# Gate's probability carried with the scattered rows and multiplied in by ScalarE; layer 0's outputs gathered by DMAs that add into x

## The chip, the cores and the metric

The kernel runs on one core of a Trainium2 chip. The metric is the time of one execution on the device in microseconds (us). An execution that the hardware profiler recorded gives a span, from the first to the last instruction, and everything that is said by engine, line or stage. The engines are called by the profile's names: PE (TensorE's matrix multiplications; PEld are its weight loads), DVE (VectorE), ACT (ScalarE), POOL (GpSimd) and SP (SyncE, which only issues DMAs here).

## What is computed

Two layers, each a graph part and a feed-forward part, on x of 128 graphs x 64 nodes x 256 channels in float32 (8192 nodes). The change lies in layer 0's feed-forward part, a mixture of eight experts of which each node takes one:

```
x = x + graph_part_0(layernorm(x), adj)
xf = layernorm(x)                               # 8192 x 256
H = gelu(xf @ W1 + b1)                          # 8192 x 1024
probs = softmax(H @ Wg + bg)                    # 8 experts
assign = argmax(probs)
out = sum over e of where(assign == e, probs[:, e] * (H @ Wd[e] + bd[e]), 0)
x = x + out
x = x + graph_attention_1(layernorm(x), adj)    # layer 1, 64 x 64 attention per graph
x = x + experts_1(layernorm(x), edge_index)     # 4 experts, two of them for each node
```

So a node's output is its expert's product, plus that expert's bias, times the largest probability of its own softmax.

## The kernel before

The 8192 nodes are 64 tiles of 128 (P); four tiles make a group (GR), so there are 16 groups. x stays in the core's own memory, SBUF, all the time (`x`, P x 64 x 256). The kernel goes through stages, and the instructions of each engine are put in order by a scheduler that works on the program when it is built: what stands later in the code can be ahead on an engine if nothing forbids it. `tc.issue_after(v)` holds an instruction behind v in that order. Buffers come from pools with a fixed number of each tile (`bufs`); who takes a buffer again waits for its last reader.

**Layer 0, groups (0 to 620 us).** `graph` does the graph part. `gated` (from L678) does the first half of the experts: it normalizes a group, multiplies by W1 with gelu (`hidden`, L457), turns the gelu rows back to one node per partition (`turned`, L705, copied by ACT into `rows`, two tiles of P x 4 x 512), and computes the gate. At L742 and L743 the largest probability of each node goes into `psel` (P x 64, kept to the end). The node's place among its expert's rows (`pos`, L768) is counted with matrix multiplications. Then POOL scatters the gelu rows by indirect DMA (L773): for each tile two DMAs, each of 128 rows of 512 floats, into the DRAM tensors `hrows0` and `hrows1`, which hold the rows sorted by expert.

**The turn to the slots (620 to 650 us).** After the last group SP fills the 128 rows past each expert's end with zeros (L837, 16 DMAs, of which each expert has two), and the last four slots' rows of `yrows` (L844). DVE computes which expert and which rows each of the slots has (`slot_e`, `slot_t`), and where each node's output will stand in `yrows` (`row_y`).

**The slots (650 to 1000 us).** A slot is 128 sorted rows of one expert; 68 are always done (`slots(0, SURE)`), four more under a condition on the device. `slots` has `load` (L939: two DMAs on SP's queue bring a slot's 128 x 1024 gelu rows into `hin`, of which there are three buffers), `turn` (PE transposes them in eight pieces, L951, four to a PSUM tile; ACT copies each four to `hTt`, L954), sixteen matrix multiplications of an expert's weights (L969; eight of them in the code, which the profile counts twice), the addition of the bias by DVE (L977), and the write of y to DRAM on SP's queue (L978). In the code load(t + 2) and turn(t + 1) stand ahead of slot t's multiplications. Beside them DVE sorts the edges' keys for layer 1 (`keys.finish`, `keys.count`), and PE counts them (L311); both are held behind the bias addition of the slot before.

**Layer 1's graph part (1001 to 1380 us).** A loop of steps (`for s in range(n_steps)`) runs five streams of groups at different lags: `back` (lag 0), `first`, `second`, `combine` and `tables`. `back(g)` brings layer 0's outputs home: for each of a group's four tiles POOL gathers 128 rows of 256 floats from `yrows` by indirect DMA into a buffer `yin` (L1180; six buffers, shared with later work), DVE multiplies it by `psel` and adds it to x (L1195), and DVE takes the sums for the normalization (`raw_stats`, L1172). The additions of some groups are held behind the factors or scores of an earlier group (`ahead`). After each pair of steps `make_factors` turns the sums into scale and shift. From step 12 on, matrix multiplications of layer 1's experts (`units`, L1101 and L1111) are put between, and after these stages PE has work to the end (2120 us).

Of the kernel before, what the change touches and what calls it, by code (L numbers as in the profile page):

```python
# [82 lines left out]
def kernel(  # L83
# [99 lines left out]
    n_left = n_chunks * n_chunk + n_firsts // PER + n_extra  # L183
    dram = ctx.enter_context(tc.tile_pool(name="dram", bufs=1, space=DRAM))
    left = dram.tile([n_left, P, PER], F32, name="left")
    hrows = [dram.tile([E0 * NROW, HALF], F32, name=f"hrows{i}") for i in range(FD // HALF)]
    yrows = dram.tile([NSLOT * P, D], F32, name="yrows")
    psel = const.tile([P, NT], F32, name="psel")
    row_y = const.tile([P, NT], I32, name="row_y")
    on = const.tile([P, NT, 64], U8, name="on")  # L190
    cnt = const.tile([P, NT], F32, name="cnt")
# [230 lines left out]
    with tc.tile_pool(name="w0", bufs=1, reuse_waits="tile") as w0, tc.tile_pool(name="kp", bufs=1, reuse_waits="tile") as kp:  # L422
# [29 lines left out]
        with tc.tile_pool(name="bg1", bufs=1, reuse_waits="tile") as bg1, tc.tile_pool(  # L452
# [19 lines left out]
            with tc.tile_pool(name="b2", bufs=1, reuse_waits="tile") as b2, tc.tile_pool(  # L472
# [205 lines left out]
                def gated(g):  # L678
# [21 lines left out]
                        S.copy(zT[:, c, :], tz)  # L700
                        yield
                    hTs = []
                    rows = [b2.tile([P, GR, HALF], F32, name=f"rows{i}") for i in range(FD // HALF)]

                    def turned(q):  # L705
                        th = psb.tile([P, GR * P], F32, name="tz")
# [32 lines left out]
                    yield  # L739
                    V.reciprocal(sm, sm)  # L740
                    V.tensor_tensor(pr, pr, sm.unsqueeze(2).to_broadcast([P, GR, E0]), ALU.mult)
                    best = psel[:, GR * g : GR * g + GR]  # L742
                    V.tensor_reduce(best, pr, AX.X, ALU.max)  # L743
                    V.tensor_tensor(pr, pr, best.unsqueeze(2).to_broadcast([P, GR, E0]), ALU.is_equal)
                    V.tensor_tensor(pr, pr, order.unsqueeze(1).to_broadcast([P, GR, E0]), ALU.mult)
                    V.tensor_reduce(m, pr, AX.X, ALU.max)
# [72 lines left out]
            with tc.tile_pool(name="bg3", bufs=1, reuse_waits="tile") as bg3:  # L819
                pk = psg0.tile([P, GR * P], F32, name="ms")  # L820
                nc.tensor.matmul(pk[:, 0:E0], ones, run[:, NG, 0, :], start=True, stop=True)
                full = bg3.tile([P, E0], I32, name="full")

                none = bg3.tile([P, D], F32, name="none")
                nc.gpsimd.memset(none, 0.0)
                V.tensor_tensor(full, pk[:, 0:E0], base, ALU.add)
                _, ends = nc.values_load_multi_w_load_instructions(
                    full[0:1, :],
                    engines=(mybir.EngineType.SP,),
                    min_val=0,  # L830
                    max_val=E0 * NROW - P,
                    skip_runtime_bounds_check_because="an expert has N nodes at most",
                )
                for e in range(E0):
                    for rows in hrows:
                        alone(
                            nc.sync.dma_start(  # L837
                                rows[bass.ds(ends[e], P), :].rearrange("p (k f) -> p k f", f=D),
                                none.unsqueeze(1).to_broadcast([P, HALF // D, D]),
                            )  # L840
                        )

                for t in range(SURE, NSLOT):
                    nc.sync.dma_start(yrows[t * P : t * P + P, :], none)  # L844
                full = bg3.tile([P, E0], I32, name="fullt")
                V.tensor_scalar(full, pk[:, 0:E0], float(P - 1), None, ALU.add)
                V.tensor_scalar(full, full, 7, None, ALU.logical_shift_right)
                tiles = bg3.tile([P, E0], F32, name="tiles")
                V.tensor_copy(tiles, full)
                end = bg3.tile([P, E0], F32, name="end")  # L850
                V.tensor_copy(end[:, 0:1], tiles[:, 0:1])
                for e in range(1, E0):
                    V.tensor_tensor(end[:, e : e + 1], end[:, e - 1 : e], tiles[:, e : e + 1], ALU.add)
                iota_s = bg3.tile([P, NSLOT], F32, name="iota_s")
                nc.gpsimd.iota(
                    iota_s, pattern=[[1, NSLOT]], base=0, channel_multiplier=0, allow_small_or_imprecise_dtypes=True
                )

                posf = bg3.tile([P, NT], F32, name="posf")
                V.tensor_copy(posf, pos)  # L860
                move = bg3.tile([P, NT], F32, name="move")
                shift = bg3.tile([P, E0], F32, name="shift_y")
                V.tensor_scalar(shift, tiles, float(P), -float(NROW), ALU.mult, ALU.add)
                V.tensor_copy(row_y, posf)
                for e in range(1, E0):
                    V.tensor_scalar(move, posf, float(e * NROW), shift[:, e - 1 : e], ALU.is_ge, ALU.mult)
                    V.tensor_tensor(row_y, row_y, move, ALU.add)

                V.tensor_scalar(more_slots, end[:, E0 - 1 : E0], float(SURE), None, ALU.is_gt)
                most = bg3.tile([P, 1], F32, name="most")  # L870
                V.tensor_scalar(most, end[:, E0 - 1 : E0], -1.0, None, ALU.add)
                V.tensor_scalar(iota_s, iota_s, most, None, ALU.min)
                past = bg3.tile([P, NSLOT, E0], BF16, name="past")
                V.tensor_tensor(
                    past,
                    iota_s.unsqueeze(2).to_broadcast([P, NSLOT, E0]),
                    end.unsqueeze(1).to_broadcast([P, NSLOT, E0]),
                    ALU.is_ge,
                )
                es = bg3.tile([P, NSLOT], F32, name="es")  # L880
                V.tensor_reduce(es, past, AX.X, ALU.add)
                V.tensor_copy(slot_e, es)
                V.tensor_tensor(past, past, tiles.unsqueeze(1).to_broadcast([P, NSLOT, E0]), ALU.mult)
                first = bg3.tile([P, NSLOT], F32, name="first")
                V.tensor_reduce(first, past, AX.X, ALU.add)
                V.tensor_tensor(iota_s, iota_s, first, ALU.subtract)
                V.scalar_tensor_tensor(es, es, float(NROW // P), iota_s, ALU.mult, ALU.add)
                V.tensor_scalar(es, es, 0.0, float(E0 * NROW // P - 1), ALU.max, ALU.min)
                last = V.tensor_copy(slot_t, es).ins
# [6 lines left out]
        if True:  # L896
            with tc.tile_pool(name="bs", bufs=3, reuse_waits="tile") as bs, tc.tile_pool(
# [15 lines left out]
                def slots(first, end):  # L913
# [3 lines left out]
                    def load(t):  # L917

                        if t % GR == 0:
# [14 lines left out]
                            )  # L934
                            for k in range(GR):
                                found[t + k] = at[k], ex[k]
                        h = loaded[t] = bz.tile([P, FD], F32, name="hin")
                        for i, rows in enumerate(tiles_of_rows):
                            nc.sync.dma_start(  # L939
                                h[:, i * HALF : i * HALF + HALF],  # L940
                                rows[bass.ds(found[t][0], 1)].rearrange("s p f -> (s p) f"),
                            )

                    def turn(t):

                        h = loaded.pop(t)
                        hT = turned[t] = bt.tile([P, NH, P], F32, name="hTt")
                        for i in range(0, NH, GR):
                            th = pst.tile([P, GR * P], F32, name="th")
                            for k in range(GR):  # L950
                                nc.tensor.transpose(  # L951
                                    th[:, k * P : k * P + P], h[:, (i + k) * P : (i + k) * P + P], ident
                                )
                            S.copy(hT[:, i : i + GR, :].rearrange("p q n -> p (q n)"), th)  # L954
# [4 lines left out]
                    for t in range(first, end):  # L959
# [15 lines left out]
                            )  # L975
                        y = bs.tile([P, D], F32, name="y")
                        add_bd = V.tensor_tensor(y, py, bd, ALU.add).ins  # L977
                        nc.sync.dma_start(yrows[t * P : t * P + P, :], y)  # L978
                        yield add_bd

# [169 lines left out]
    with ExitStack() as of_c:  # L1150
# [22 lines left out]

        def back(g):

            ys = []
            for k in range(GR):
                t = GR * g + k
                y = by.tile([P, D], F32, name="yin")
                nc.gpsimd.indirect_dma_start(  # L1180
                    y, None, yrows, bass.IndirectOffsetOnAxis(ap=row_y[:, t : t + 1], axis=0)
                )
                ys.append(y)


            if PART <= g <= FIRST:
                ahead = made["factors"]
            elif FIRST < g <= 2 * FIRST:
                ahead = made["scores"]
            else:  # L1190
                ahead = None
            for k in range(GR):
                t = GR * g + k
                with tc.issue_after(ahead) if ahead is not None else ExitStack():
                    V.scalar_tensor_tensor(x[:, t, :], ys[k], psel[:, t : t + 1], x[:, t, :], ALU.mult, ALU.add)  # L1195
                raw_stats(0, k, x[:, t, :])
                yield

        def transposed(g, norm):
# [976 lines left out]
```

## Time and profile before

| | |
|---|---|
| median of 12 executions | 2122.68 us (2118.01 to 2131.57) |
| the profiled execution | 2121.72 us, its span 2120.0 us, PE's granted clock 0.955 |
| PE | 1937.3 us busy, 91% of the span |
| PE's weight loads | 1394.6 us, 66% |
| DVE | 1341.0 us, 63% |
| ACT | 941.7 us, 44% |
| POOL | 491.3 us, 23% |
| bytes moved by DMA | 274.94 MB, mean 130 GB/s |

The shares are means over stages with different limits; by stage, in us busy:

| stretch (us) | PE | DVE | ACT | POOL | PE's clock | DMA share |
|---|---|---|---|---|---|---|
| 0 to 100 | 80.07 | 76.01 | 65.62 | 14.63 | 1.00 | 0.51 |
| 200 to 300 | 92.10 | 87.47 | 65.38 | 25.32 | 0.98 | 0.29 |
| 600 to 640 | 16.69 | 15.48 | 10.15 | 14.86 | 0.74 | 0.46 |
| 660 to 996 | 335.97 | 276.99 | 70.05 | 0.00 | 1.00 | 0.52 |
| 1001 to 1211 | 157.48 | 158.26 | 114.18 | 63.29 | 0.78 | 0.27 |
| 1300 to 1400 | 97.56 | 66.13 | 43.24 | 0.59 | 1.00 | 0.48 |
| 1800 to 2000 | 200.00 | 74.41 | 75.46 | 53.87 | 1.00 | 0.87 |

A group's line in the profile names line, engine and operation, the tile written, an arrow and the tiles read, and the count; after the bar come busy us, mean ns of one, and the idle time of the engine just before them with what ended it ("<-PE th L951" is PE's write of `th` at line 951). A line of the timeline has start and duration in us, engine, line, operation, tiles and count; in brackets the idle time before it. SPq is SP's own sequencer, whose DMA instructions are the issue of a transfer and not the transfer itself. L numbers are lines of the kernel before.

### The profile page before, as it was taken

The page shows a single profiled execution, that of the slowest core. Times are in us where ns is not written, and L with a number is a line of the kernel's source. Part 1 is how long each engine was busy: PE and PEld are TensorE (multiplying, and loading weights), DVE is VectorE, ACT ScalarE, POOL GpSimd, SP SyncE. Part 2 cuts the span into 40 slices and gives each one's busy share as a digit, 9 for nine tenths or more (in the row PEclk, how much of TensorE's full clock was granted, in tenths as well). Part 3 has the DMA queues.
Part 4 walks back from the last instruction along what each step waited for, and adds up shares of the span by engine and source line. Part 5 has one row for each costly group of instructions (what it writes and reads, how often), then busy time and mean ns, then how long its engine had stood idle before and what let it go on. Part 6 is the DMA issues. An engine that isn't in the chain of part 4 may idle for free. (4 is left out here: it accounts for less than half of the span.)

```text
span 2120.0 us, 32316 instructions
## 1 busy us (share of the span) xinstructions
PE 1937.3 (91%) x10422; PEld 1394.6 (66%) x10422; DVE 1341.0 (63%) x4346; ACT 941.7 (44%) x1721; POOL 491.3 (23%) x528
## 2 busy tenths in 40 slices
PE   7889999899957999997678999989999999999999
PEld 5444445454436989897446676757777767888876
DVE  6878988843126888885697655846778451334435
ACT  4867766766641222221365655322333333333332
POOL 2013121223220000000530100015555552303223
PEclk9999999999988999999777899999999999999999
DMA  8023222234226554544214111472222147878943
GB/s 239 27 93 118 83 96 95 87 117 165 89 111 210 153 166 153 156 157 118 76 52 136 61 43 42 142 205 62 48 58 64 42 138 250 291 255 271 293 129 100
DMA packets 229376, 274.94 MB, mean 130 GB/s; under 512 B 57937, under 2 KB 173521, under 8 KB 229201
## 3 DMA queue, kind: packets, MB, share of 16 engines
q1 hardware_dynamic: 194288, 212.26, 32.4%
q0 software_dynamic: 24064, 60.22, 9.0%
q8 instruction: 88, 1.44, 0.3%
q10 hardware_dynamic: 10848, 0.30, 0.3%
q14 instruction: 88, 0.71, 0.1%
HBM read 159.40 MB, written 113.22 MB: 129 GB/s over the span
## 5 line engine op out<-in xcount | busy, mean ns | idle before, releaser
L464 PE MATMUL ph<-zT,w 128*128 128x512 f32 x512 | 250.2, 614 | 4.8 <-ACT zT L700 3.4
L969 PE MATMUL py<-wd,hTt 128*128 x1088 | 247.4, 381 | 0.0
L969 PEld LDWEIGHTS py<-wd,hTt 128*128 128x128 f32 x1088 | 202.7, 191 | 25.0
L954 ACT COPY hTt<-th 128x512 f32<-128x512 f32 x136 | 73.2, 589 | 299.6 <-PE th L951 299.6
L1578 POOL DMA_INDIRECT got<-tsrc,esrc x144 | 152.2, 1057 | 213.0 <-DMA zslots<-none 84.5
L1111 PE MATMUL py<-w,hT 128*128 128x256 f32 x800 | 192.6, 392 | 9.3 <-DVE y L1115 5.2
L773 POOL DMA_INDIRECT hrows<-rows,pos x128 | 126.6, 989 | 307.1 <-issue 188.7
L1101 PE MATMUL ph<-zT,w 128*128 128x512 f32 x400 | 184.1, 601 | 0.0
L1111 PEld LDWEIGHTS py<-w,hT 128*128 128x128 f32 x800 | 151.5, 194 | 40.8 <-issue 11.4
L1180 POOL DMA_INDIRECT yin<-yrows,row_y x64 | 63.3, 989 | 489.1 <-SPq L1024 370.5
L464 PEld LDWEIGHTS ph<-zT,w 128*128 128x128 f32 x512 | 94.7, 197 | 105.9 <-issue 89.4
L1105 ACT ACTIVATE hT<-ph,b 128x512 f32<-128x512 f32 x100 | 68.6, 687 | 185.0 <-PE ph L1101 176.5
L2055 ACT ACTIVATE hT<-ph,b1e 128x256 f32<-128x256 f32 x152 | 71.9, 473 | 173.0 <-PE ph L2051 101.7
L2051 PE MATMUL ph<-zTp,w1e 128*128 128x256 f32 x608 | 137.6, 379 | 3.7 <-DMA w1e<-in_L_ffn_W_dram 3.7
L2064 PE MATMUL py<-w,hT 128*128 x608 | 137.5, 379 | 0.0
L2072 DVE TENSOR_TENSOR y<-py,b2e 128x256 f32<-128x256 f32 x76 | 32.1, 424 | 152.5 <-PE py L2064 136.7
L2051 PEld LDWEIGHTS ph<-zTp,w1e 128*128 128x128 f32 x608 | 115.4, 190 | 19.8 <-issue 4.3
L626 PE MATMUL pre<-wd 128*128 128x512 f32 x256 | 123.9, 601 | 1.8 <-ACT wd L612 1.3
L2064 PEld LDWEIGHTS py<-w,hT 128*128 128x128 f32 x608 | 112.7, 190 | 13.8
L467 ACT ACTIVATE hT<-ph,b 128x512 f32<-128x512 f32 x128 | 87.8, 686 | 76.1 <-PE ph L464 60.3
L1101 PEld LDWEIGHTS ph<-zT,w 128*128 128x128 f32 x400 | 73.4, 191 | 71.4 <-issue 70.3
L201 DVE TENSOR_TENSOR one<-iota_l,pb 128x2048 bf16<-128x2048 bf16 x96 | 116.6, 1214 | 0.2
(411 smaller groups left out, 3779.2 us busy)
## 6 DMA issues: line engine op xcount, KB each, us to landing
hin<-hrows SPq DMA_DIRECT2D x136, 256.0 KB
w1e<-in_L_ffn_W_dram SPq DMA_DIRECT2D x38, 512.0 KB
yin<-ystore SPq DMA_DIRECT2D x24, 512.0 KB
ystore<-y SPq DMA_DIRECT2D x80, 128.0 KB
zslots<-none SPq DMA_DIRECT2D x38, 256.0 KB
zin<-zslots SPq DMA_DIRECT2D x38, 256.0 KB
yslots<-y SPq DMA_DIRECT2D x76, 128.0 KB
bd<-in_L_ffn_bd_dram SPq DMA_DIRECT2D x68, 128.0 KB
```

What stands on the lines that cost most here:

```text
L201: V.tensor_tensor(o, numbers.unsqueeze(1).to_broadcast(shape), of.rearrange("p (j e) -> p j e", e=2).unsqueeze(2).to_broadcast(shape), ALU ...
L464: nc.tensor.matmul(ph, w1[:, c, q * P : q * P + P], zT[:, c, :], start=(c == 0), stop=(c == 1))
L467: gelus.append(S.activation(hT, ph, AF.Gelu, bias=b1[:, q : q + 1]).ins)
L626: nc.tensor.matmul(pre, xnT[:, c, n * P : n * P + P], wcat[:, c, :], start=(c == 0), stop=(c == 1),)
L773: nc.gpsimd.indirect_dma_start(to, bass.IndirectOffsetOnAxis(ap=pos[:, t : t + 1], axis=0), of[:, k, :], None)
L954: S.copy(hT[:, i : i + GR, :].rearrange("p q n -> p (q n)"), th)
L969: nc.tensor.matmul(py, hT[:, q, :], wd[:, bass.ds(e, 1), q, :].rearrange("p e f -> p (e f)"), start=(q == 0), stop=(q == NH - 1),)
L1101: nc.tensor.matmul(ph, w1[:, e, c, q * P : q * P + P], zT[:, c, :], start=(c == 0), stop=(c == 1))
L1111: nc.tensor.matmul(py, hTs[q][:, k * P : k * P + P], w2[:, e, q, :], start=(q == 0), stop=(q == NH1 - 1))
L1578: nc.gpsimd.indirect_dma_start(got, None, tsrc, bass.IndirectOffsetOnAxis(ap=esrc[:, b, at : at + 1], axis=0))
L2051: nc.tensor.matmul(ph, w1e[:, c, q * P : q * P + P], zT[:, c, :], start=(c == 0), stop=(c == 1))
L2064: nc.tensor.matmul(py, hTs[q][:, k * P : k * P + P], w2[:, e, q, :].rearrange("p e f -> p (e f)"), start=(q == 0), stop=(q == NH1 - 1),)
```

## The change

`hrows1` and its row tile become one float wider (513), and the added column holds the node's largest probability: it is copied there from `best`, a small tile that replaces `psel`, and so goes out with the scatter. The zero fill of the rows past an expert's end is done for the old columns as before and, by eight further DMAs, for the added column. A slot's load brings 1025 columns; after the bias has been added ACT multiplies y by the last column of the slot's rows, and then y is written. `loaded.pop(t)` moves from `turn` to that place. In `back` the gather's target is x itself, with an addition in the DMA; the buffers `yin`, DVE's multiplication and addition, and the order that held them are gone there, and the sums that remain are held in their place.

```diff
-    hrows = [dram.tile([E0 * NROW, HALF], F32, name=f"hrows{i}") for i in range(FD // HALF)]
+    wide = [HALF + (i == FD // HALF - 1) for i in range(FD // HALF)]
+    hrows = [dram.tile([E0 * NROW, n], F32, name=f"hrows{i}") for i, n in enumerate(wide)]
     yrows = dram.tile([NSLOT * P, D], F32, name="yrows")
-    psel = const.tile([P, NT], F32, name="psel")
...
-                    rows = [b2.tile([P, GR, HALF], F32, name=f"rows{i}") for i in range(FD // HALF)]
+                    rows = [b2.tile([P, GR, n], F32, name=f"rows{i}") for i, n in enumerate(wide)]
...
-                    best = psel[:, GR * g : GR * g + GR]
+                    best = bg2.tile([P, GR], F32, name="best")
                     V.tensor_reduce(best, pr, AX.X, ALU.max)
+                    V.tensor_copy(rows[-1][:, :, HALF], best)
...
                     for rows in hrows:
                         alone(
                             nc.sync.dma_start(
-                                rows[bass.ds(ends[e], P), :].rearrange("p (k f) -> p k f", f=D),
+                                rows[bass.ds(ends[e], P), 0:HALF].rearrange("p (k f) -> p k f", f=D),
                                 none.unsqueeze(1).to_broadcast([P, HALF // D, D]),
                             )
                         )
+                    alone(nc.sync.dma_start(hrows[-1][bass.ds(ends[e], P), HALF : HALF + 1], none[:, 0:1]))
...
-                        h = loaded[t] = bz.tile([P, FD], F32, name="hin")
+                        h = loaded[t] = bz.tile([P, FD + 1], F32, name="hin")
                         for i, rows in enumerate(tiles_of_rows):
                             nc.sync.dma_start(
-                                h[:, i * HALF : i * HALF + HALF],
+                                h[:, i * HALF : i * HALF + wide[i]],
                                 rows[bass.ds(found[t][0], 1)].rearrange("s p f -> (s p) f"),
                             )
...
-                        h = loaded.pop(t)
+                        h = loaded[t]
...
                         add_bd = V.tensor_tensor(y, py, bd, ALU.add).ins
+                        prob = loaded.pop(t)[:, FD : FD + 1]
+                        S.activation(y, y, AF.Copy, scale=prob)
                         nc.sync.dma_start(yrows[t * P : t * P + P, :], y)
...
-            ys = []
             for k in range(GR):
                 t = GR * g + k
-                y = by.tile([P, D], F32, name="yin")
                 nc.gpsimd.indirect_dma_start(
-                    y, None, yrows, bass.IndirectOffsetOnAxis(ap=row_y[:, t : t + 1], axis=0)
+                    x[:, t, :],
+                    None,
+                    yrows,
+                    bass.IndirectOffsetOnAxis(ap=row_y[:, t : t + 1], axis=0),
+                    compute_op=ALU.add,
                 )
-                ys.append(y)
...
             for k in range(GR):
-                t = GR * g + k
                 with tc.issue_after(ahead) if ahead is not None else ExitStack():
-                    V.scalar_tensor_tensor(x[:, t, :], ys[k], psel[:, t : t + 1], x[:, t, :], ALU.mult, ALU.add)
-                raw_stats(0, k, x[:, t, :])
+                    raw_stats(0, k, x[:, GR * g + k, :])
                 yield
```

## The prediction

> **What bounds the kernel now.** I read the page first, then busy time by stage, then the timeline of the stages that the diff touches: the turn from layer 0's first part to its experts (620 to 650 us), the 68 slots (650 to 1000 us) and the start of layer 1 (1001 to 1211 us, where the outputs are gathered).
>
> ```profile
> L954 ACT COPY hTt<-th 128x512 f32<-128x512 f32 x136 | 73.2, 589 | 299.6 <-PE th L951 299.6
> L1180 POOL DMA_INDIRECT yin<-yrows,row_y x64 | 63.3, 989 | 489.1 <-SPq L1024 370.5
> ```
>
> ```profile
> 850.00:900.00 50.00, 50.00 (x478) 45.06 (x477) 42.42 (x106) 10.74 (x20) 0.00 (x0) 1.00 0.52 154
> 1000.00:1050.00 50.00, 24.98 (x92) 16.38 (x92) 29.48 (x105) 14.81 (x33) 29.75 (x30) 0.66 0.28 82
> 1050.00:1100.00 50.00, 37.02 (x152) 23.85 (x152) 45.91 (x156) 34.69 (x66) 18.11 (x18) 0.90 0.17 48
> ```
>
> The columns of the second fence are the stretch, its length, busy us of PE, PE's weight loads, DVE, ACT and POOL, then granted clock, DMA share and GB/s. In the slots PE never rests (50.00 of 50 us at clock 1.00), and ACT is idle four fifths of the time, always waiting for PE. From 1050 to 1100 us DVE is the full engine (45.91 of 50). So time taken from DVE there is worth something, and work given to ACT in the slots looks free, by its share. One slot in the timeline:
>
> ```profile
> 851.30 1.07 PE L951 MATMUL th<-ident,hin 128*128 128x128 f32 x8
> 851.70 0.41 DVE L977 TENSOR_TENSOR y<-py,bd 128x256 f32<-128x256 f32 x1
> 852.03 1.07 ACT L954 COPY hTt<-th 128x512 f32<-128x512 f32 x2 [3.77 <-PE th L951]
> 852.13 0.33 SPq L978 DMA_DIRECT2D yrows<-y  x1
> 852.21 3.62 PE L969 MATMUL py<-wd,hTt 128*128 x16
> 852.71 0.86 SPq L939 DMA_DIRECT2D hin<-hrows  x2
> 853.78 0.34 SPq L966 DMA_DIRECT2D bd<-in_L_ffn_bd_dram  x1
> ```
>
> A slot lasts 5.04 us: the writes of y go from 659.20 to 996.7 us, 67 steps. What is to be seen is the order: PE turns a slot one slot before it multiplies it, and SP sends a load as soon as the turning has freed a buffer. In the order of the built program, SP sends the load of slot t+5 after y of slot t is written, and PE turns slot t+2 ahead of multiplying t+1. A load has more than two slots to land, and no slot past the second waits for one.
>
> **The slots, after.** hin has 3 buffers. Before, hin of slot t is free once PE has turned it. Now ACT's multiplication by its last column reads it, and that comes after slot t's matmuls. The order of the changed program shows what follows. SP: write of y(t), then load(t+3). ACT: both copies of slot t+2, then the multiplication of slot t. PE: matmuls of t+2, then (in part just inside them) the turning of t+3. Every link is real: load(t+3) needs the buffer that multiplication t frees; multiplication t stands behind the copies of t+2; those need the turning, and so the landing, of load(t+2). So load, turn, copy, multiply, write and next load form a ring that is run once **per slot**. Its length, from SP's write of y:
>
> - write of y to the next load's start: 852.13 to 852.71, 0.58 us.
> - that start to the landing of the load's second half. Nearest rows:
>
> ```profile
> 646.51 3.03 SPq L939 DMA_DIRECT2D hin<-hrows  x6
> 649.24 2.79 PE L951 MATMUL th<-ident,hin 128*128 128x128 f32 x12 [9.98 <-DMA hin<-hrows]
> ```
>
> ```profile
> 1763.36 0.41 SPq L2022 DMA_DIRECT2D w1e<-in_L_ffn_W_dram  x1
> 1767.70 3.69 PE L2051 MATMUL ph<-zTp,w1e 128*128 128x256 f32 x16 [3.74 <-DMA w1e<-in_L_ffn_W_dram]
> ```
>
> The first 256 KB half let PE go 2.73 us after its issue; the second is issued 0.53 us later (0.86 for two, 0.33 for one), so 3.26 us if it takes no longer. The 512 KB of w1e took 4.34 us. I take the middle, 3.8.
> - four transposes and the way to ACT: 851.30 to 852.03, 0.73 us.
> - second copy to the multiplication's start: 1.07 less 0.59, 0.48 us.
> - the multiplication, 128x256: 0.47 us, as the same Copy with a scale takes at L634; between 0.40 (a plain copy, L1127) and 0.60 (L1069).
> - ACT's end to SP: 852.11 to 852.13, 0.02 us.
> - late issues: 13 of the 68 pairs of loads took 1.05 to 2.37 us in place of 0.86, 11.6 us in all, 0.17 a slot. They were hidden and would be no more.
>
> Sum: 0.58 + 3.8 + 0.73 + 0.48 + 0.47 + 0.02 + 0.17 = 6.25 us against 5.04. Loads 3 to 67 are in the ring, so 65 x 1.21 = **+79 us**. By the short ends (3.26, 0.40, no late issue) a slot is 5.47 us, +28; by the long ones (4.34, 0.60) 6.92, +122. PE's own 5.04 us then lies beside the ring with 1.2 us of idle time in each slot. ACT's 68 x 0.47 = 32 us cost nothing as work; it is their place behind the copies that costs.
>
> The Trainium skill has another price for the landing: "DMA: Bandwidth & Descriptors", on the anatomy of one DMA, fits 2.0 us plus bytes over 436 GB/s (its fit is for POOL's queue). That is 2.60 us for a half; with the row's 0.53 ahead of it, 3.13 in place of 3.8, and 65 x 0.54 = 35 us less. The first load's 2.73 agrees with it; w1e's 4.34 is above its 3.2.
>
> **The turn to the slots.** PE stands still from the last group to 649.24 ("9.98 <-DMA hin"). In it SP issues 16 zero fills (630.65 to 642.42, 0.74 us each) and 4 of 128 rows (0.55 each), then the first load, which waits for their landing. The change adds 8 fills of 128 rows by 4 bytes in that row: 8 x 0.55 to 0.74 = 4.4 to 5.9, I take **+5 us**. The scatters' rows grow from 2048 to 2052 bytes; POOL's time for one doesn't follow the row (1057 ns for 80 bytes at L1578, 989 for 1 KB and for 2 KB), so nothing, at most 1 us for the last eight. Gate's added copy on DVE (128x4, some 0.2 us, 16 times) lies beside a PE that is 92% busy there; once, in the last group, it is on the path: 0.2. At the end of the slots the last multiplication adds 0.5.
>
> **The gathers.** 64 additions on DVE go (475 ns each, 0.40 apart when packed); 30 of them start between 1038 and 1112 us, where DVE is busy 66.88 of 74 us. At most 12 us go; PE, ACT and their handoffs come next, as DVE's idle pieces show, so I take **-8**. The 22 before 1038 lie under gathers (8 at 1.25 us, then the landing) and a stretch where engines wait for "remote"; the 12 after 1112 beside PE. Nothing. The gathers lose their wait for a free buffer (29 us of POOL's idle time to 1120) and run ahead: 64 x 1.25 = 80 us, done by 1085, always before layer 1's step needs them. What a gather that adds costs, no row shows. If it is as the plain one, it hides behind 20 us for each pair of steps (8 gathers, 10 us). If it takes twice that, the first pair starts 10 us later and the rest still fit. So -12 to +10.
>
> **Sum**, against the profiled execution's own 2121.72 us (span 2120.0; the median of the twelve is 2122.68): 79 + 5 + 0.2 + 0.5 - 8 = +76.7, so 2198 us.
>
> **Rivals.**
> - *The loads are hidden all the same.* Place: the landing. All terms but it and the late issues make 2.28 us, so if both halves land within 2.76 us of the first's issue, PE's 5.04 still sets the slot. For it: the first half did land in 2.73. Against it: the second is issued 0.53 later. Then +5.7 and -8: 2119 us, not slower; -12 gives 2115.
> - *The adding gather is slow.* It decides from some 2.6 us each (8 in 21 us); 64 at 4 us take 256 us where layer 1's steps leave 210 (1001 to 1211): 46 + 8 more, 2252 us. For it: a second operand is read on the way. Against: DMA is busy for 0.28 of 1000 to 1050 us.
> - *PE's clock falls with the gaps.* The row of 1000 to 1050 us shows 0.66. At 0.72, PE's 5.04 us become 7.0: 65 x 0.75 more, 2247 us. Against: at 1.2 us of idle in 6.25 PE is 80% busy, and the first 100 us of the kernel show 80% at clock 1.00. The skill's "TensorE: Matmul & The Clock Gate" (part 1) sets the gate's window at some 3.4 us, longer than these gaps, and so speaks against it too.
> - *The change doesn't do what it says.* Its order shows the gathers with x as their target and no addition on DVE, so this is out.
>
> **How the numbers follow.** Forecast 0.78, hidden loads 0.08, slow gather 0.09, clock 0.05. The forecast's own ends are 2121.7 + 28 + 4.4 - 12 = 2142 and 2121.7 + 122 + 7 + 10 = 2261; I set 2145 to 2260, which takes in the two slower rivals at the prices above. Faster by over 0.2% 0.04, within 0.2% (about what a measurement of this kernel can tell from no change) 0.04, slower 0.92.
>
> **What would show it.** Right: writes of y some 6.2 us apart; PE about 80% busy from 660 to 1070 at clock near 1.00, its transposes waiting for "DMA hin" for about 65 x 1.2 us; the first load some 5 us later after the fills; gathers in one row at 1.25 us; DVE less busy in layer 1's start. Wrong: writes of y 5.0 us apart (the landing is shorter than the rows say), a clock well under 1 in the slots, or bn_stats waiting for the gathers past the first eight.

## The result and the profile after

The changed kernel takes 2230.82 us (median of 11 executions, 2224.68 to 2238.1) against 2122.73 us before (46 executions): 1.0514 times as long, with an interval of 1.0499 to 1.0528. That is 108 us; the forecast was +76.7. The profiled execution after has a span of 2237.1 us at a mean PE clock of 0.951, so its span is 117.1 us longer than that of before. Cut at marks that both timelines have, this growth lies here (the factors are `fac`, written 13 times in layer 1's first part, L1333 before, L1334 after):

| from | to | before, us | after, us | growth | forecast |
|---|---|---|---|---|---|
| start | end of the last scatter on POOL | 630.3 | 633.5 | +3.2 | 0 |
| | first write of y | 28.9 | 40.4 | +11.5 | +5.2 |
| | last write of y (67 steps) | 337.5 | 429.5 | +92.0 | +79 |
| | first gather | 4.6 | 3.6 | -1.1 | +0.5 |
| | last of the 13 factors | 369.4 | 376.4 | +7.0 | -8 |
| | end | 749.3 | 753.7 | +4.5 | 0 |

The first and last rows are spread between executions: in the eleven kernels profiled below the last scatter ended between 627 and 637 us and the last stretch took 750 to 762, with no edit that is made there.

The groups of the page that answer to those of before, and two more:

```profile
L971 PE MATMUL py<-wd,hTt 128*128 x1088 | 266.2, 389 | 36.0 <-DVE y L979 27.4
...
L956 ACT COPY hTt<-th 128x512 f32<-128x512 f32 x136 | 79.5, 586 | 349.0 <-PE th L953 346.9
L1182 POOL DMA_INDIRECT x<-yrows,row_y x64 | 100.6, 1572 | 492.2 <-SPq L1028 473.0
...
L979 DVE TENSOR_TENSOR y<-py,bd 128x256 f32<-128x256 f32 x68 | 28.9, 425 | 165.8 <-DMA bd<-in_L_ffn_bd_dram 113.0
L953 PE MATMUL th<-ident,hin 128*128 128x128 f32 x544 | 86.2, 283 | 46.0 <-DMA hin<-hrows 45.3
```

The transposes now wait for hin, as foreseen. The fourth row was not foreseen: the addition of the bias waits 113 us for its bias. A gather holds POOL for 1572 ns in the mean, where the plain one took 989. By stage, in the columns of before:

```profile
850.00:900.00 50.00, 43.49 (x382) 36.27 (x381) 35.44 (x83) 13.04 (x24) 0.00 (x0) 1.00 0.40 127
1106.00:1156.00 50.00, 19.43 (x74) 12.72 (x74) 19.62 (x75) 12.26 (x28) 41.07 (x27) 0.66 0.51 73
1156.00:1206.00 50.00, 33.74 (x144) 24.06 (x144) 33.89 (x123) 29.78 (x63) 42.08 (x27) 0.76 0.51 70
```

In the slots PE no longer is busy all the time, but its clock stays at 1.00. At the start of layer 1 DVE does less (19.62 us, where the first 50 us of before from 1001 us had 30.48), yet POOL is busy most of the time and the DMA share is 0.51 at 73 GB/s, where it was 0.29 at 85. One slot of the timeline, from write of y to write of y:

```profile
880.51 0.33 SPq L982 DMA_DIRECT2D yrows<-y  x1
...
881.08 0.86 SPq L941 DMA_DIRECT2D hin<-hrows  x2
...
882.17 0.33 SPq L968 DMA_DIRECT2D bd<-in_L_ffn_bd_dram  x1
...
884.76 0.60 PE L953 MATMUL th<-ident,hin 128*128 128x128 f32 x4
...
885.40 0.59 ACT L956 COPY hTt<-th 128x512 f32<-128x512 f32 x1 [0.23 <-PE th L953]
885.41 0.42 DVE L979 TENSOR_TENSOR y<-py,bd 128x256 f32<-128x256 f32 x1 [2.00 <-DMA bd<-in_L_ffn_bd_dram]
...
885.88 0.51 ACT L981 ACTIVATE y<-y,hin 128x256 f32<-128x256 f32 x1
...
886.41 0.33 SPq L982 DMA_DIRECT2D yrows<-y  x1
```

Two chains lead from the first line to the last. One is the predicted ring: load of hin, transposes, second copy (885.40 + 0.59), multiplication. The other goes by way of bd: SP issues the bias of slot t+1 only behind the loads of hin, 1.66 us after the write; it is there at 885.41, and then come addition and multiplication. They end within 0.2 us of each other. Averaged over the first 64 steps from write to write, the first is 0.67 (write to load) + 5.11 (load to the end of the second copy) + 0.18 (to the multiplication) + 0.51 + 0.03 = 6.5 us, the second 1.93 (write to bd's issue) + 3.51 (to the addition) + 1.05 (to the next write) = 6.5 us. Over all 67 steps, of which the last few have no load left to wait for, a slot takes 6.41. Which of the two ends last differs from slot to slot: of 65 multiplications, 43 start within 0.1 us of the end of their addition, when the copies have been done, 13 wait for the second copy after the addition has been done, and in 9 both end together. So it is the chain by way of bd, which was not foreseen, that ends last in most slots.

### The profile page after: what moved, and what is told of

Same layout as the page of the kernel before. It is cut to its first block, busy times and chain, and to the rows that moved or that the text cites. A ratio compares the mean times of both kernels' runs of the same rounds, so it can differ in the third digit from the quotient of the medians.

```text
span 2237.1 us, 32572 instructions
## 1 busy us (share of the span) xinstructions
PE 1965.9 (88%) x10422; PEld 1397.9 (62%) x10422; DVE 1326.8 (59%) x4298; ACT 979.5 (44%) x1789; POOL 529.5 (24%) x528
## 3 DMA queue, kind: packets, MB, share of 16 engines
q0 software_dynamic: 30208, 60.26, 10.1%
## 5 line engine op out<-in xcount | busy, mean ns | idle before, releaser
L971 PE MATMUL py<-wd,hTt 128*128 x1088 | 266.2, 389 | 36.0 <-DVE y L979 27.4
L971 PEld LDWEIGHTS py<-wd,hTt 128*128 128x128 f32 x1088 | 198.2, 192 | 64.0 <-ACT hTt L956 33.7
L956 ACT COPY hTt<-th 128x512 f32<-128x512 f32 x136 | 79.5, 586 | 349.0 <-PE th L953 346.9
L1182 POOL DMA_INDIRECT x<-yrows,row_y x64 | 100.6, 1572 | 492.2 <-SPq L1028 473.0
L464 PEld LDWEIGHTS ph<-zT,w 128*128 128x128 f32 x512 | 94.2, 196 | 106.2 <-issue 87.8
L979 DVE TENSOR_TENSOR y<-py,bd 128x256 f32<-128x256 f32 x68 | 28.9, 425 | 165.8 <-DMA bd<-in_L_ffn_bd_dram 113.0
L953 PE MATMUL th<-ident,hin 128*128 128x128 f32 x544 | 86.2, 283 | 46.0 <-DMA hin<-hrows 45.3
```

Source lines behind the costliest of these rows:

```text
L464: nc.tensor.matmul(ph, w1[:, c, q * P : q * P + P], zT[:, c, :], start=(c == 0), stop=(c == 1))
L953: nc.tensor.transpose(th[:, k * P : k * P + P], h[:, (i + k) * P : (i + k) * P + P], ident)
L971: nc.tensor.matmul(py, hT[:, q, :], wd[:, bass.ds(e, 1), q, :].rearrange("p e f -> p (e f)"), start=(q == 0), stop=(q == NH - 1),)
L1182: nc.gpsimd.indirect_dma_start(x[:, t, :], None, yrows, bass.IndirectOffsetOnAxis(ap=row_y[:, t : t + 1], axis=0), compute_op=ALU.add,)
```

## The experiments: the slots

Theory: two rings set the slot, by way of hin and by way of bd. Rivals: ACT's added work, the wider rows, or one of the rings alone. All ratios are to the time before, run beside the kernel on the same chip; slot lengths are from the first to the last of 68 writes of y.

**prob_early.** POOL copies the column out of hin, so hin is free again once it has been turned.

```diff
                         hT = turned[t] = bt.tile([P, NH, P], F32, name="hTt")
+                        prob = probs[t] = bt.tile([P, 1], F32, name="prob")
+                        nc.gpsimd.tensor_copy(prob, h[:, FD : FD + 1])
...
-                        prob = loaded.pop(t)[:, FD : FD + 1]
-                        S.activation(y, y, AF.Copy, scale=prob)
+                        S.activation(y, y, AF.Copy, scale=probs.pop(t))
```

> POOL, idle in the slots, copies each slot's column of probabilities out of hin, so that hin is free once PE has turned it and POOL has copied; ACT multiplies by the copy. Theory (the multiplication holds hin and so closes a ring of load, turn, copy, multiply, write, next load, run once a slot): the ring is gone, the loads go ahead again, and a slot takes 5.04 to 5.2 us in place of 6.41; 2139 to 2150 us. Rival 1 (ACT's own work, 1.6 us a slot and its place in the queue, is what costs): 6.4 us a slot still, 2231. Rival 2 (the wider rows make the loads slow): over 6 us a slot, with PE's transposes waiting for the loads.

Measured: 2141.68 us, ratio 1.0076 (1.0051 to 1.0100); a slot takes 5.03 us. Its stretch:

```profile
850.00:900.00 50.00, 50.00 (x478) 45.05 (x477) 42.98 (x104) 15.24 (x30) 8.23 (x10) 1.00 0.51 158
```

PE is full again, with the same multiplication on ACT, the same 2052-byte rows and the same DMAs. So neither ACT's work nor the rows' width costs anything in the slots; that hin is held does.

**bd_first.** The bias is issued ahead of the loads of hin.

```diff
-                        if t + 2 < end:
-                            load(t + 2)
-                        if t + 1 < end:
-                            turn(t + 1)
-                        e, hT = found.pop(t)[1], turned.pop(t)
+                        e = found.pop(t)[1]
                         bd = bs.tile([P, D], F32, name="bd")
                         nc.sync.dma_start(bd, f0_bd[bass.ds(e, 1), :].to_broadcast([P, D]))
+                        if t + 2 < end:
+                            load(t + 2)
+                        if t + 1 < end:
+                            turn(t + 1)
+                        hT = turned.pop(t)
```

> In each slot the load of bd is issued ahead of the load of hin, nothing else. As built, bd of slot t+1 then goes ahead of the write of y(t), and ACT multiplies slot t one pair of copies earlier, so that both rings are loosened: that by way of bd (write of y, two loads of hin, bd, its landing, addition, multiplication: 0.57 + 1.09 + 3.24 + 0.42 + 0.51 and handoffs, 5.9 us) is cut, that by way of hin (6.25 us) is run once for two slots. Theory (these two rings set the slot): some 5.05 to 5.4 us a slot, 2139 to 2163. Rival 1 (a slot is set by the landing of hin itself, whatever the order): over 6 us a slot, 2205 to 2231. Rival 2 (the long issues on SP, 1 to 2 us, set it): 5.5 to 6.0 us.

Measured: 2154.52 us, ratio 1.012 (1.0078 to 1.0161); a slot takes 5.21 us, no addition waits for bd, and the transposes wait 3.7 us for hin in all from 700 to 990 us. hin is held as long as in the changed kernel; the order of the queues alone gives back most of the loss. But the edit loosens both rings, so two more kernels close one each.

**copies_held.** The ring of bd alone: ACT's copies of slot t+2 are queued behind the multiplication of slot t.

```diff
-                            S.copy(hT[:, i : i + GR, :].rearrange("p q n -> p (q n)"), th)
+                            with tc.issue_after(muls[t - 2]) if t - 2 in muls else ExitStack():
+                                S.copy(hT[:, i : i + GR, :].rearrange("p q n -> p (q n)"), th)
...
-                        S.activation(y, y, AF.Copy, scale=prob)
+                        muls[t] = S.activation(y, y, AF.Copy, scale=prob).ins
```

> The change with ScalarE's order held: the copies of slot t+2 stand behind the multiplication of slot t in place of ahead of it; SP's order is as changed. The ring by way of hin is then run once for two slots; the ring by way of bd (write of y(t), loads of hin, bd of t+1, addition, multiplication, write of y(t+1)) stays, 5.9 us. If hin's ring alone sets the slot: 5.05 to 5.2 us a slot. If both are last by turns: 5.9 to 6.0, the additions waiting for bd in nearly every slot. If bd's alone, or SP's long issues: 6.4.

Measured: 2227.46 us (one execution; the kernel before took 2123.06 beside it); a slot takes 6.32 us. From 700 to 990 us the waits show:

```profile
DVE y L980 <- DMA bd<-in_L_ffn_bd_dram: 71.6, 45, 3.3
```

In 45 of the slots there the addition waits for bd, 1.6 us in the mean, and every one of the 65 multiplications starts within 0.1 us of the end of its addition. The ring of bd alone makes 6.32 us; my 5.9 had used one short passage (3.24 us from issue to addition), where the mean of this kernel is 3.5, and 1.9 from write to issue where I had 1.66.

**no_bd_order.** The ring of hin alone: no bias is loaded or added, and the order of the changed kernel is held.

```diff
-                        bd = bs.tile([P, D], F32, name="bd")
-                        nc.sync.dma_start(bd, f0_bd[bass.ds(e, 1), :].to_broadcast([P, D]))
...
-                        add_bd = V.tensor_tensor(y, py, bd, ALU.add).ins
+                        add_bd = V.tensor_copy(y, py).ins
...
+                        with tc.issue_after(behind) if behind is not None else ExitStack():
+                            S.activation(y, y, AF.Copy, scale=prob)
```

> The ring by way of hin alone: bd is neither loaded nor added (y is a plain copy of the product, so the bias is missing from layer 0's outputs), and the order of the changed kernel is held by hand: copies of slot t+2 ahead of the multiplication of slot t on ScalarE, write of y(t) ahead of the load of t+3 on SP. If the ring of hin was as long as the prediction had it (6.25 us), a slot takes 6.2 to 6.4 us, as changed. If the ring of hin is shorter and the wait for bd set the slot of the changed kernel: 5.1 to 5.9 us, and the time falls by 33 to 88 us. If PE turns late and waits for ScalarE's copies: between, with the matmuls waiting for hTt.

Measured: 2235.05 us (one execution; the kernel before took 2128.76 beside it); a slot takes 6.39 us with one DMA fewer. A passage of it:

```profile
859.48 0.33 SPq L963 DMA_DIRECT2D yrows<-y  x1
860.41 1.27 SPq L941 DMA_DIRECT2D hin<-hrows  x2
...
862.14 0.42 DVE L986 COPY y<-py 128x256 f32<-128x256 f32 x1 [3.53 <-issue]
...
864.81 0.86 PEld L953 LDWEIGHTS th<-ident,hin 128*128 128x128 f32 x8
864.84 1.07 PE L953 MATMUL th<-ident,hin 128*128 128x128 f32 x8
...
865.56 1.07 ACT L956 COPY hTt<-th 128x512 f32<-128x512 f32 x2 [6.10 <-PE th L953]
866.19 2.89 PEld L978 LDWEIGHTS py<-wd,hTt 128*128 128x128 f32 x14 [0.53 <-ACT hTt L956]
866.20 3.07 PE L978 MATMUL py<-wd,hTt 128*128 x13 [0.29 <-ACT hTt L956]
...
866.52 0.52 ACT L962 ACTIVATE y<-y,hin 128x256 f32<-128x256 f32 x1
...
867.06 0.33 SPq L963 DMA_DIRECT2D yrows<-y  x1
```

The product is copied at 862.14, and nothing is left for y to wait for; still its multiplication starts at 866.52, behind the copies of a later slot, which wait for the transposes, which wait for the load. This passage is a long one (7.6 us, with a late second issue).

| rings closed | kernel | us a slot |
|---|---|---|
| hin and bd | the changed kernel | 6.41 |
| bd | copies_held | 6.32 |
| hin | no_bd_order | 6.39 |
| neither | bd_first, prob_early | 5.21, 5.03 |

Each ring alone gives the whole loss and either hides the other: to open one gains 2 to 6 us, to open both 80 to 93 (67 steps). The 2 to 6 us can't be told from nothing: wide_fill and plain_gather below, which leave both rings closed, take 6.36 and 6.35 us a slot.

## The experiments: the turn and the gathers

**wide_fill.** Whole rows in place of 1 KB pieces and 4-byte columns.

```diff
-                none = bg3.tile([P, D], F32, name="none")
+                none = bg3.tile([P, HALF + 1], F32, name="none")
...
-                    for rows in hrows:
-                        alone(
-                            nc.sync.dma_start(
-                                rows[bass.ds(ends[e], P), 0:HALF].rearrange("p (k f) -> p k f", f=D),
-                                none.unsqueeze(1).to_broadcast([P, HALF // D, D]),
-                            )
-                        )
-                    alone(nc.sync.dma_start(hrows[-1][bass.ds(ends[e], P), HALF : HALF + 1], none[:, 0:1]))
+                    for rows, n in zip(hrows, wide):
+                        alone(nc.sync.dma_start(rows[bass.ds(ends[e], P), :], none[:, 0:n]))
```

> The zero rows behind each expert are filled by one transfer of 128 whole rows for each half (2048 and 2052 bytes a row) in place of two transfers of 1 KB pieces and one of 4 bytes a row; 16 fills in place of 24. Theory (the 4-byte fills and the pieces at a stride of 2052 bytes are what lands late, and SP waits for the eighth transfer before): the waits of SP between fills go with them, the first load of hin comes some 8 to 12 us earlier than in the changed kernel (25.4 us after the first fill there, 15.9 before the change), and the time is 2219 to 2223. Rival 1 (only the eight issues cost): 4 to 5 us less, 2226. Rival 2 (rows of 2052 bytes make every transfer of them slow, the scatters' too): nothing less. Slots and gathers as after.

Measured: 2221.68 us, ratio 1.0438 (1.0400 to 1.0477). The first load of hin starts 18.7 us after the first fill (25.4 in the changed kernel, 15.9 before). SP's waits in the changed kernel (625 to 665 us):

```profile
SPq L838 <- DMA hrows<-none: 4.6, 5, 2.4
SPq L846 <- DMA hrows<-none: 1.7, 3, 0.8
SPq L941 <- DMA hrows<-none: 1.6, 1, 1.6
```

Before the change SP waited for no landing between its fills. The expectation that these waits go was wrong: in wide_fill SP still waits 6.7 us for fills, in place of 7.9. The stretch of the fills, before the change, in the changed kernel and in wide_fill:

```profile
631.00:647.00 16.00, 1.01 (x16) 0.95 (x16) 10.88 (x44) 0.00 (x0) 0.00 (x0) 0.50 0.93 308
```

```profile
634.00:659.30 25.30, 1.01 (x16) 0.95 (x16) 11.06 (x44) 0.00 (x0) 0.04 (x1) 0.50 1.04 194
```

```profile
634.40:653.00 18.60, 1.01 (x16) 0.95 (x16) 11.07 (x44) 0.00 (x0) 0.12 (x1) 0.50 1.03 266
```

The last two columns are DMA share and GB/s. The DMA engines are full in all three (0.93 to 1.04), and all three move the same 4.9 MB (16 x 308, 25.3 x 194, 18.6 x 266). So the turn seems to be set by the rate at which the DMA engines get the fills done, and that rate fell. The packets in the traces show where. The 4-byte packets took 0.9 us of the 16 engines' 25.3, so the columns load the engines little. The 1 KB packets took 88 ns in the mean in the changed kernel and 49 before, at nearly the same median (46 and 48): some of them took very long, up to 1.6 us.

From the first fill to the first load whole rows give back 6.7 of 9.5 us in this pair. From last scatter to first write of y it is less: 34.2 us in the mean of five kernels with whole rows (wide_fill, and four below that have it too), 39.1 in the six with the fills as changed, 28.9 before. That is 4.9 us, which rival 1 gave to the eight issues alone, so how much is issues and how much the DMA engines' rate is not shown. The time doesn't tell them apart either: by the ratios wide_fill is 16 us below the changed kernel, but 8 of these lie in the slots and the first factors, which the edit doesn't touch.

What is left was not taken apart. It isn't the columns or the pieces' size, since wide_fill has no columns and its pieces are larger than those of before; what both kernels have and that of before hasn't are the rows at a stride of 2052 bytes. One reading: the Trainium skill's "DMA: Bandwidth & Descriptors", "How a descriptor splits into AXI transactions", says that a descriptor which does not start on a multiple of 256 B fetches bytes that it does not use. At a stride of 2052 nearly all rows start off one, but on the side that is written. The trace doesn't bear this reading out: in wide_fill the packets of 2052 bytes and those of 2048 took as long as each other (medians 85 and 84 ns, means 127 and 127), with very long ones among both. The cause stays open.

**plain_gather.** The gather goes into a tile again and DVE adds it into x.

```diff
-                nc.gpsimd.indirect_dma_start(
-                    x[:, t, :],
-                    None,
-                    yrows,
-                    bass.IndirectOffsetOnAxis(ap=row_y[:, t : t + 1], axis=0),
-                    compute_op=ALU.add,
-                )
+                y = by.tile([P, D], F32, name="yin")
+                nc.gpsimd.indirect_dma_start(
+                    y, None, yrows, bass.IndirectOffsetOnAxis(ap=row_y[:, t : t + 1], axis=0)
+                )
+                ys.append(y)
...
-                    raw_stats(0, k, x[:, GR * g + k, :])
+                    t = GR * g + k
+                    V.tensor_tensor(x[:, t, :], ys[k], x[:, t, :], ALU.add)
+                raw_stats(0, k, x[:, t, :])
```

> The change without its last part: rows and slots as after, but the outputs are gathered into a tile and added into x by VectorE (128x256, tensor + tensor), as before without the probability. Theory (the adding gather is dearer than the plain one: 1.54 us of POOL in place of 0.95, so the first factors of layer 1 come later): a gather takes 0.95 us again, the stage from the first gather to the last of layer 1's first factors is some 7 us shorter than in the changed kernel (369 us against 376), and the time falls by about 7 us, to some 2224. Rival (the additions that VectorE no longer does are worth more than the dearer gather costs, and the stage's growth is of another cause): the time rises by up to 8 us, to 2231 to 2239. The slots stay at 6.4 us in both.

Measured: 2228.91 us, ratio 1.0474 (1.0436 to 1.0512), which overlaps the changed kernel's interval. A gather takes 0.95 us again, and from the first one to the last of the 13 factors it is 371.4 us. With adding gathers this stretch took 376.4 in the changed kernel and, in six other kernels that share them, 371.6 to 377.8: 374.7 in the mean of seven, against 370.8 of three with plain ones. So the adding gather costs about 4 us net, less than the expected 7 and of the other sign than the predicted 8. The seven lie in two groups, though, three at 371.6 to 372.1 and four at 376.4 to 377.8, with the same gathers; the lower group is level with the two plain ones of the changed kernels (371.4 and 371.5). What puts a kernel into one group or the other was not found, so the 4 us are a mean, and no kernel with adding gathers alone was shorter here than before (369.4). The changed kernel's waits from 1107 to 1232 us, and its queue of POOL's DMAs from 1109 to 1147 us:

```profile
DVE raw L1176 <- DMA x<-yrows,row_y: 40.4, 19, 11.7
ACT z L1073 <- DVE fac L1334: 33.0, 2, 24.7
```

```profile
q0 software_dynamic: 2971, 2.72, 52.7%
```

That queue before, from 1003 to 1041 us:

```profile
q0 software_dynamic: 1069, 2.94, 26.7%
```

DVE's first statistics and 18 more wait 40 us for gathers; over a stretch as long before (1001 to 1126 us), DVE's additions waited 9.3 us for them. In these 38 us 21 gathers made 2971 packets, 141 each, and took 16 x 38 x 0.527 / 21 = 15.3 us of DMA engine time each. The plain ones made 1069 packets at 26.7% for 23 gathers: 46 packets and 7.1 us each, for the same 128 KB.

**best_add, best_plain, best_mixed.** prob_early and wide_fill together, with the adding gather, with the plain one, and with the first 16 tiles plain and 48 adding.

```diff
+                if g < 4:
+                    y = by.tile([P, D], F32, name="yin")
+                    nc.gpsimd.indirect_dma_start(
+                        y, None, yrows, bass.IndirectOffsetOnAxis(ap=row_y[:, t : t + 1], axis=0)
+                    )
+                    ys.append(y)
+                    continue
```

> prob_early and wide_fill together, all else as changed. If the two costs add (the rings of the slots, some 89 us; the fills, some 9 us): 0.4% under prob_early, at 1.003 times the time before, a slot at 5.03 us, the first write of y some 33 us after the last scatter. If the slots' ring only hid the fills: as prob_early, 1.007.

> As best_add, with the plain gather and VectorE's addition. Theory (the adding gather is dearer by the first factors' 4.7 us and by VectorE's waits for it, and gives back about as much by the additions saved): within 5 us of best_add, the first factors of layer 1 at 16 us after the first gather in place of 20.7. Rival (the saved additions are worth the predicted 8 us): 8 us slower than best_add. Rival (the dear gather costs its whole +7): 7 us faster.

> As best_add, but the first 16 tiles are gathered plainly and added by VectorE, the other 48 by adding gathers. Theory (what the adding gather costs is that its pace of 1.84 us falls behind layer 1's need in its first 70 us): the first factors at 16 us, the third at under 58 us in place of 71 after the first gather, and 3 to 8 us less than best_add: at the time before or just under it. Rival (the gathers' load on the DMA engines, or the clock, costs it): as best_add.

Measured, on one chip: best_add 2134.63 us, ratio 1.005 (1.0032 to 1.0069); best_plain 2129.89, 1.003 (1.0013 to 1.0046); best_mixed 2123.28, 1.001 (0.9992 to 1.0027). The slots take 5.03 us in all three. From the first gather to the last factor: 377.8, 371.5 and 368.8 us. So the additions saved seem to be worth something, some 2 us in this stretch, if the first tiles don't wait for the slow gathers. The steps I had named were wrong, though: the first factors come at 18.1 us (expected 16), the third at 63.5 (expected under 58).

**best_mixed2, best_late.** Only 8 plain tiles; and the spare rows of outputs zeroed inside the slots, from a tile of their own.

```diff
-                if g < 4:
+                if g < 2:
```

```diff
-                for t in range(SURE, NSLOT):
-                    nc.sync.dma_start(yrows[t * P : t * P + P, :], none[:, 0:D])
...
+                nil = c0.tile([P, D], F32, name="nil")
+                nc.gpsimd.memset(nil, 0.0)
                 for t, unit in enumerate(slots(0, SURE)):
+                    if t == 2:
+                        for spare in range(SURE, NSLOT):
+                            nc.sync.dma_start(yrows[spare * P : spare * P + P, :], nil)
```

> As best_mixed, but only the first 8 tiles are gathered plainly, the other 56 by adding gathers. Theory (only the first pair's pace counts): the first factors at 16 us after the first gather, the second by 36, the third by 58, and 0 to 4 us less than best_mixed, 0.998 to 1.001 of before. Rival (VectorE's waits come back with the earlier adding gathers): the third at over 60 us, and as best_add, 1.003 to 1.005.

> As best_mixed2, and the four zero rows of outputs past the sure slots are written from a tile of their own after the third slot's start, no longer between the zero fills and the first load. Theory (they stand in SP's row and on the DMA engines ahead of the first load): the first load of hin 2 to 4 us nearer to the last fill, and 2 to 4 us less than best_mixed2, under the time before if that is level with it. Rival (the load waits for the fills' landing anyway): no difference.

Measured: best_mixed2 2132.91 us, ratio 1.0024 (1.0010 to 1.0038); best_late 2130.77, 1.0018 (0.9997 to 1.0038). The third factors come at 67.0 us in best_mixed2, so its theory falls; the whole stretch is 368.8 us all the same, as with 16 tiles. Without the four spare rows the first load comes 5.8 us after the last fill's issue, where best_mixed2 has 6.3, and the first write of y 31.1 us after the last scatter, where it has 33.3; the times don't tell the two apart. The load came 0.5 us nearer and not 2 to 4, because it then waits 4.0 us for the fills' landing, where in best_mixed2 it waits 1.0: here the rival was right. **No version was faster than before**: the best is level with it.

## Why the prediction was right, and where its sizes were off

The direction, the predicted ring and the range were right (2231 in 2145 to 2260); the forecast of 2198 was 33 us low, and a second ring that it didn't have ends last in most slots.

- *The ring of the slots, 6.25 us.* The mechanism is shown: with hin freed early the slot is 5.03 us, with the ring closed alone 6.39. The landing term held: 3.8 + 0.73 + 0.48, with 0.17 for late issues, made 5.18 us from load to multiplication, measured 5.29 in the changed kernel and 5.31 in no_bd_order, where this ring is alone. The multiplication was 0.51, not 0.47, and write to load 0.67, not 0.58. PE was 87% busy from 850 to 900 us by the profile, not 80.
- *What the ring left out.* I listed SP's row as "write of y(t), then load(t+3)" and stopped there. Behind it stands bd of t+1, which before had been two slots ahead; the loads' wait for hin is also bd's wait. It makes a second ring of 6.3 us, and of the 65 multiplications 43 waited for this one and 13 for the predicted one. That it changed the forecast little is luck: the two rings are of nearly the same length. By an estimate from copies_held, with loads landed in 2.76 us, but bd as it was measured there, my rival "hidden loads" would have come to 6.3 us a slot and not 5.04.
- *The slots' sum, +79*: measured +92. The difference is 0.16 us on each slot and two slots more than the 65 counted.
- *The turn, +5.* Mis-sized: +11.5 in this pair, +10.2 in the mean of six profiles with the same fills (28.9 us before, 37.2 to 40.9 after, from last scatter to first write). I priced issues on SP; the DMA engines were already 0.93 busy in that stretch, and their rate fell from 308 to 194 GB/s. How the growth divides between the two is not shown.
- *The gathers, -8.* Mis-sized and of the wrong sign: +7.0 in this pair, +4 in the mean. I took 1.25 us a gather "always ahead"; it is 1.54 on POOL and 1.84 from one to the next, 118 us for 64 in place of 80, and the statistics did wait for it, which the prediction named as the sign that this step is wrong. The bound of twice the plain price (+10) held it. Of the additions that I counted at nothing, 16 and not 22 start before 1038 us and 18 and not 12 after 1112, which leaves the sum as it is.
- *Rivals.* The clock stayed at 1.00 in the slots. The adding gather came nowhere near the 2.6 us from which it decides. The Trainium skill's landing price ("DMA: Bandwidth & Descriptors", anatomy of one DMA) of 3.13 us would have given, as an estimate, a slot of 5.58 us and +35 in the slots, which is 44 us less than +79, and not 35 less as the prediction has it; the trace's 5.29 us for the whole link is on the side of 3.8.

## What to carry to other kernels

When a change lets a buffer go later, write down everything that is queued behind the load that waits for it, on the same queue: the next transfer there becomes later with the load (here the 128 KB of a bias), and its consumer may close a second ring, here of the same length. To free such a buffer, copy out the small thing that holds it. Before transfers are priced by their issues alone, look whether the DMA engines are full in that stretch. Price work that is moved into a DMA by the DMA's pace, since an engine that waits for the DMA at the head of its queue can lose what the move was to save.

## What the runs showed of the hardware that was not expected

An indirect gather that adds into SBUF took POOL 1.54 us where the plain one took 0.95, and 15.3 us of DMA engine time in place of 7.1, for 128 rows of 1 KB. Counted over all 64 gathers, an adding one made 144 packets, 128 of 1 KB and 16 of 4 bytes, and a plain one 48, 32 of 4 KB and 16 of 4 bytes. That is the whole growth of POOL's packets (30208 less 24064 = 6144 = 64 x 96).

The 4.9 MB that moved in the stretch of the zero fills went at 308 GB/s with 1 KB pieces at a stride of 2048 bytes, at 266 with whole rows, half of them of 2052 bytes, and at 194 with 1 KB pieces, half of them at a stride of 2052, and eight 4-byte columns of 128 rows, each time with the DMA engines full.
